# Graph network kernel: one wait in front of a group's eight matmuls, one release behind them, and the two paths as two `If`s

## The chip, the cores and the metric

The kernel runs on one core of one Trainium2 chip. The metric is the device time of one execution in microseconds (us). The engines are named as the profile names them: PE multiplies matrices, PEld is its weight load, DVE and ACT are the vector and the scalar engine, POOL is GpSimd, SP issues most of the plain transfers. A trailing q (SPq, POOLq, DVEq) is an engine's own instruction queue.

## What is computed

Four graph layers follow one another on 6250 nodes with 256 features and 100000 edges, sorted by destination. Cut to what matters:

```python
h = relu(layernorm(x)); x = x + L0(h)   # 8-head attention over edges, then a feed-forward part
h = relu(layernorm(x)); x = x + L1(h)   # msg = h[src] * filter(edge); sum by dst; two projections
h = relu(layernorm(x)); x = x + L2(h)   # one-head attention over edges
h = relu(layernorm(x)); x = x + L3(h)   # graph convolution: sum of h[src] by dst, scaled, plus bias
```

Each layer gathers one table row for every edge by `src` and sums the rows, weighted, by `dst`.

## The kernel before

**Groups.** The edges are cut into G = 98 groups of 1024. A group is J = 8 tiles of 128 edges. For every tile one indirect DMA, issued by POOL (`gather`, line 129; its line in the profile is L130), brings 128 table rows from DRAM into SBUF. Then eight matmuls add the eight tiles up in one PSUM tile, by multiplying the rows with a one-hot matrix that says which of 128 neighbouring nodes an edge ends at. Each float32 matmul shows as two passes in the profile, so a group's sum is 16 entries. The sums of overlapping node windows are then put together for each block of 128 nodes (`sum_block`), and the block goes on through the layer's dense part.

**Four stages.** There is one loop over the groups for each layer; the text calls them stages 0 to 3.

- Stage 0 (lines 792 to 827): `rows0` (L184) gathers into slices of `xbuf`, NV = 6 groups deep; `logits0` (L746) reads a column of all eight tiles, L816 multiplies the rows in place by the attention values on DVE, `one_hot0` (L731) and `one_hot_t` (L725, the instruction at L729) build one-hot tiles, and `sum_window` (L666, matmul L670) sums. `rows0` of the first four groups stands before the branch.
- Between stages 0 and 1 lies the feed-forward part (`feed_forward` and lines 831 to 921), with no gathers.
- Stage 1 (lines 978 to 1036): gathers go into slices of `big`, NH = 12 groups deep. `filters` (L954) makes three PSUM tiles of edge filters on PE (L960), for tiles 0 to 2, 3 to 5 and 6 to 7; three DVE multiplications (L1005) put them on the rows; the matmuls (L1008) sum. Then DVE works on the edge features (`ea`, L1010 and L1011), on the block that is done (`out1`, L971), on `row` (L1026), on the next one-hot (`one_hot1`, L968) and adds the sum to `agg` (L1035).
- Stage 2 (lines 1108 to 1121): `rows2` (L1049) gathers into a pool of five buffers; `one_hot2` (L1064) reads a column of all eight tiles (L1068), takes an exponential on ACT (L1072) and builds eight scaled one-hot tiles (L1075); `sum_window` sums; `out2` (L1079) and `table3_row` (L1101) finish a block.
- Stage 3 (lines 1143 to 1160): gathers go into a pool of six buffers; the matmuls (L1154) take the tiles in the order 7, 6, ..., 0; the one-hot tiles (`one_hot3`, L1127, instruction L1130) are built one group ahead; `end3` (L1134) writes the result.

**What sets the order.** Inside `tc.manual_schedule()` each engine runs its instructions in the order of the code. Engines are held to each other by semaphores alone. The framework places a wait wherever an instruction reads what another engine or a DMA wrote, or writes where another still reads. It tracks slices: a gather into tile j of `xbuf` or `big` waits for the matmul that read tile j some groups before, and matmul j waits for gather j and for the DVE instruction that wrote what it reads. The gathers use eight DMA semaphores in turn, so a group's eight gathers have eight different ones. Buffers from a pool (stages 2 and 3) are given back as a whole, after the last reader. POOL issues nothing but gathers in the loops, so it runs ahead of the other engines as far as the buffers allow.

**The two paths.** At line 309 a flag is read into a register, `general`, on every engine. Lines 1444 to 1449 run `fast()`, described above, when it is 0, and else `slow()`, a general version. With these inputs the fast path runs. Inside it a smaller `If` (L1058) guards a rare case and is not taken.

Of the kernel before, what the change touches and what calls it, by code (L numbers as in the profile page):

```python
# [13 lines left out]
OP = mybir.AluOpType  # L14
# [3 lines left out]
P = 128  # L18
J = 8
W = 128  # L20
D = 256
H = 8
HD = D // H
FF = 512
FL = 128
VR = D + H + 1
TR = D + 2
# [8 lines left out]
def tile_gnn(ctx: ExitStack, tc: tile.TileContext, a: dict, out: bass.AP, N: int):  # L36
# [11 lines left out]
    nc = tc.nc  # L48
# [78 lines left out]
        nc.vector.reciprocal(o, o)  # L127

    def gather(rows, table, idx, j):
        nc.gpsimd.indirect_dma_start(  # L130
            out=rows, out_offset=None, in_=table,
            in_offset=bass.IndirectOffsetOnAxis(ap=idx[:, j:j + 1], axis=0))

    def norm_stats(b0, b1):
        for b in range(b0, b1):
# [45 lines left out]
    AHEAD = 4  # L181
    vrows = [xbuf[:, i * J * VR:(i + 1) * J * VR].rearrange("p (j r) -> p j r", j=J) for i in range(NV)]

    def rows0(g):  # L184
        for j in range(J):
            gather(vrows[g % NV][:, j, :], vt, src_i[:, g * J:(g + 1) * J], j)

    sct = dram.tile([NP, 2 * H], F32, name="sct")
    with ExitStack() as l0:
# [455 lines left out]
    def fast():  # L645
# [17 lines left out]

            return [(g, HW * g - OFF - P * b) for g in range(max(0, 2 * b - 1), min(G, 2 * b + 3))]

        def sum_window(pool, oh, rows, n):  # L666

            s = ps("S", [P, n])
            for j in range(J):
                nc.tensor.matmul(s, oh[:, j, :], rows[:, j, :], start=j == 0, stop=j == J - 1)  # L670
            ws = pool.tile([P, n], F32, name="ws", bufs=6)
            nc.scalar.activation(ws, s, AF.Copy)  # L672
            return ws

        def sum_block(sums, b, n):

# [21 lines left out]
        with tc.tile_pool(name="e0", bufs=2) as ep:  # L698

            scw = ep.tile([P, NB, 2, 2 * H], F32, name="scw", bufs=1)  # L700
            for odd in range(2):
                for b0, b1 in ((0, 32), (32, NB)):
# [6 lines left out]
                    else:  # L709
# [5 lines left out]
            place = ep.tile([P, G], F32, name="place", bufs=1)  # L715
            nc.gpsimd.iota(place, pattern=[[HW, G]], base=-OFF, channel_multiplier=1,
                           allow_small_or_imprecise_dtypes=True)
            sums, drows, tos, dgs, ohs, vs, ms, mts = {}, {}, {}, {}, {}, {}, {}, {}

            def loads0(g):  # L720
                if g < G:
# [9 lines left out]
            def one_hot0(g):  # L731
                if g < G:
                    ohs[g] = ep.tile([P, J, P], F32, name="oh")
                    for j in range(J):
                        nc.vector.tensor_scalar(ohs[g][:, j, :], iota, rel[:, g * J + j:g * J + j + 1],
                                                None, OP.is_equal)

            def of_dst(g):

# [52 lines left out]
            with tc.manual_schedule():  # L792
                for g in range(2):
                    loads0(g)
                one_hot_t(0)
                one_hot0(0)
                of_dst(0)
                for g in range(G + 2):
                    vg = vrows[g % NV]
                    if AHEAD <= g < G:  # L800
                        rows0(g)
                    loads0(g + 2)
                    for b in blocks_done(g):
                        vs[b] = ep.tile([P, H, HD], F32, name="v")
                        nc.sync.dma_start(vs[b], vt[b * P:(b + 1) * P, 0:D].rearrange("p (h c) -> p h c", c=HD))
                    if g == 6:
                        made(of1)
                    if g == 8:
                        made(of2)
                    summed = [(b, sum_block(sums, b, VR)) for b in blocks_done(g - 1)]  # L810
                    projected = [(b, project0(b)) for b in blocks_done(g - 2)]
                    if g < G:
                        ex = logits0(g)
                        one_hot_t(g + 1)
                        vals = vg[:, :, 0:D].rearrange("p j (h c) -> p j h c", c=HD)
                        nc.vector.tensor_tensor(vals, vals, ex[:, :, :, None].to_broadcast([P, J, H, HD]),  # L816
                                                OP.mult)
                    of_dst(g + 1)
                    for b, s in summed:
                        attn0(b, s)  # L820
                    if g < G:
                        sums[g] = sum_window(ep, ohs[g], vg, VR)
                    for b, s in summed:
                        turn0(b)
                    one_hot0(g + 1)
                    for b, t in projected:
                        residual0(b, t)
# [103 lines left out]
        with tc.tile_pool(name="e1", bufs=2) as ep, Psum("ps1", S=2, A=3, B=1, C=1, K=1) as ps:  # L931
# [5 lines left out]
                nc.sync.dma_start(wr3[33 * i + 32:33 * i + 33, i, :], a["L1_gnn_b_r2m"][None, :])  # L937

            agg = ep.tile([P, HW * (G - 1) + P], F32, name="agg", bufs=1)
            rbs, eas, ohs, parts, normed = {}, {}, {}, {}, {}  # L940

            def loads(g):

# [10 lines left out]
            def filters(g):  # L954

                parts[g] = []
                for q in range(3):
                    n = min(3, J - 3 * q)
                    t = ps("A", [P, n, FL])
                    nc.tensor.matmul(t, rbs[g][0:33 * n, g % 2, q, :], wr3[0:33 * n, 0:n, :],  # L960
                                     start=True, stop=True)
                    parts[g].append((slice(3 * q, 3 * q + n), t))

            def one_hot1(g):
# [13 lines left out]
            with tc.manual_schedule():  # L978
# [6 lines left out]
                for g in range(G + 2):  # L985
                    hg = hgs[g % NH]
                    if g < G:
                        for j in range(J):
                            gather(hg[:, j, :], ht1, src_i[:, g * J:(g + 1) * J], j)
                    loads(g + 2)  # L990
                    added = []
                    for b in blocks_done(g - 1):
# [8 lines left out]
                            nc.tensor.transpose(t[:, k, :], normed[b][:, k * P:(k + 1) * P], ident)  # L1001
                        turned.append((b, t))
                    if g < G:
                        for js, t in parts[g]:
                            nc.vector.tensor_tensor(hg[:, js, :], hg[:, js, :], t, OP.mult)  # L1005
                        s = ps("S", [P, P])
                        for j in range(J):
                            nc.tensor.matmul(s, hg[:, j, :], ohs[g][:, j, :], start=j == 0, stop=j == J - 1)  # L1008
                        ea = eas[g]
                        nc.vector.tensor_tensor(ea, ea, wa[:, None, :].to_broadcast([P, J, FL]), OP.mult)  # L1010
                        nc.vector.tensor_reduce(te[:, g * J:(g + 1) * J], ea, AX.X, OP.add)  # L1011
# [32 lines left out]
        brow = on_all(wp, "L3_gnn_b", D)  # L1044
        bufs2, ahead = 5, 4
        with tc.tile_pool(name="e2", bufs=2) as ep:
            vgs, sums, normed = {}, {}, {}

            def rows2(g):  # L1049
                vgs[g] = ep.tile([P, J, TR], F32, name="vg", bufs=bufs2)  # L1050
                for j in range(J):
                    gather(vgs[g][:, j, :], xt2, src_i[:, g * J:(g + 1) * J], j)

            with tc.manual_schedule():
                for g in range(ahead):
# [8 lines left out]
            def one_hot2(g):  # L1064

                gs = slice(g * J, (g + 1) * J)
                al = ep.tile([P, J], F32, name="al")
                nc.vector.tensor_tensor(al[:, :, None], vgs[g][:, :, D:D + 1], te[:, gs][:, :, None], OP.add)  # L1068
                leaky(al, al, 0.01)
                nc.vector.tensor_tensor(al, al, shift[:, gs], OP.subtract)  # L1070
                ex = ep.tile([P, J], F32, name="ex")
                nc.scalar.activation(ex, al, AF.Exp)  # L1072
                oh = ep.tile([P, J, P], F32, name="oh")
                for j in range(J):
                    nc.vector.tensor_scalar(oh[:, j, :], iota, rel[:, g * J + j:g * J + j + 1],  # L1075
                                            ex[:, j:j + 1], OP.is_equal, OP.mult)
                return oh

            def out2(b, s):  # L1079

# [27 lines left out]
            with tc.manual_schedule():  # L1108
                for g in range(G + 2):
# [2 lines left out]
                    summed = [(b, sum_block(sums, b, TR)) for b in blocks_done(g - 1)]  # L1112
                    turned = [(b, turned2(normed[b])) for b in blocks_done(g - 2)]
                    if g < G:
                        oh = one_hot2(g)
                    for b, s in summed:
                        normed[b] = out2(b, s)
                    if g < G:
                        sums[g] = sum_window(ep, oh, vgs[g], TR)
                    for b, hb in turned:  # L1120
                        table3_row(b, hb)

# [1 line left out]
        with tc.tile_pool(name="e3", bufs=2) as ep, tc.manual_schedule():  # L1124
            sums = {}

            def one_hot3(g):  # L1127
                oh = ep.tile([P, J, P], F32, name="oh")
                for j in range(J):
                    nc.vector.tensor_scalar(oh[:, j, :], iota, rel[:, g * J + j:g * J + j + 1], None,  # L1130
                                            OP.is_equal)
                return oh

            def end3(b, s):  # L1134
                r0, r1 = b * P, min(N, (b + 1) * P)
# [4 lines left out]
                if r1 > r0:  # L1140
                    nc.sync.dma_start(out[r0:r1, :], y[0:r1 - r0, :])

            oh = one_hot3(0)
            for g in range(G + 1):
                if g < G:
                    vg = ep.tile([P, J, D], F32, name="vg", bufs=6)
                    for j in range(J):
                        gather(vg[:, j, :], xt3, src_i[:, g * J:(g + 1) * J], j)
                summed = [(b, sum_block(sums, b, D)) for b in blocks_done(g - 1)]
                if g < G:  # L1150

                    s = ps("S", [P, D])
                    for j in range(J):
                        nc.tensor.matmul(s, oh[:, J - 1 - j, :], vg[:, J - 1 - j, :], start=j == 0, stop=j == J - 1)  # L1154
                    if g + 1 < G:
                        oh = one_hot3(g + 1)
                    sums[g] = ep.tile([P, D], F32, name="ws", bufs=6)
                    nc.scalar.activation(sums[g], s, AF.Copy)
                for b, s in summed:
                    end3(b, s)  # L1160
# [280 lines left out]
                if r1 > r0:  # L1441
                    nc.sync.dma_start(out[r0:r1, :], y[0:r1 - r0, :])

    with tc.If(general < 1) as path:
        with ExitStack() as fctx:
            fast()
    with path.Else():
        with ExitStack() as fctx:
            slow()

# [53 lines left out]
```

## Time and profile before

| | us |
|---|---|
| five runs: median (lowest to highest) | 4511.63 (4508.82 to 4512.8) |
| the profiled execution: its own time | 4513.57 |
| the profiled execution: span from first to last instruction | 4511.8 |
| busy: PE / POOL / PEld / DVE / ACT | 3129.7 / 3070.7 / 2393.0 / 2102.2 / 624.1 |
| stage 0, from the start of its first gather to the end of its last | 180.4 to 1204.5 |
| stage 1, likewise | 1496.1 to 2479.3 |
| stage 2, likewise | 2498.6 to 3492.9 |
| stage 3, likewise | 3510.7 to 4496.4 |
| mean granted PE clock | 0.806 of full speed |

A line of groups reads: line, engine, operation, output<-inputs, count | busy us, mean ns of one | idle us just before them, and what ended most of that idle time. A line of the timeline reads: start, duration in us, engine, line, operation, count, and in brackets the idle time before it and who ended it. A line of waits reads: who waited for whom, us in total, times, longest in us. The busy time of POOL in a gather is the time that the engine spends on issuing it; the rows land later.

### The profile page before, as it was taken

How to read it: one execution, taken by the hardware profiler on the slowest of the kernel's cores; microseconds unless marked ns; L12 is line 12 of the kernel's file. 1: busy time of each engine (PE TensorE's matmuls, PEld its weight loads, DVE VectorE, ACT ScalarE, POOL GpSimd, SP SyncE). 2: the span in 40 equal slices, each digit the busy share in tenths (PEclk: the TensorE clock that was granted, in tenths of full speed). 3: DMA queues.
4: the chain of work that ended last, by engine and by line, in shares of the span. 5: the costliest groups of instructions: out<-in, count | busy, mean ns of one | idle time of the engine just before them, and what ended most of it. 6: DMA issues, size and time to landing. Idle time of an engine off the chain costs nothing.

```text
span 4511.8 us, 42644 instructions
## 1 busy us (share of the span) xinstructions
PE 3129.7 (69%) x12132; PEld 2393.0 (53%) x12133; DVE 2102.2 (47%) x6391; ACT 624.1 (14%) x1559; POOL 3070.7 (68%) x3215
## 2 busy tenths in 40 slices
PE   7689888888897666666666566666666556566565
PEld 4377777777645544445545344545444444444444
DVE  5476655565524566666767333333333222222222
ACT  3211010010124100000000122222222000000000
POOL 0377777777501677777777677777777677777776
PEclk9888888888898777777777787878778787787888
DMA  3355555555500444444444344444444333333333
GB/s 105 114 178 169 161 160 159 161 162 161 153 0 15 117 122 126 123 129 125 123 126 115 89 111 112 112 111 112 111 112 111 96 112 111 111 112 111 111 111 100
DMA packets 258746, 536.81 MB, mean 119 GB/s; under 512 B 65096, under 2 KB 144966, under 8 KB 258502
## 3 DMA queue, kind: packets, MB, share of 16 engines
q0 software_dynamic: 137984, 364.28, 29.3%
q1 hardware_dynamic: 107750, 156.85, 11.4%
q10 hardware_dynamic: 12768, 12.85, 0.9%
q8 instruction: 103, 1.69, 0.2%
q14 instruction: 141, 1.16, 0.1%
HBM read 504.57 MB, written 29.15 MB: 118 GB/s over the span
## 4 chain that ended last, share of the span: by engine, by line
PE 33%; POOL 28%; issue 15%; DMA 12%; DVE 9%; ACT 2%; DVEq 0%; POOLq 0%; ACTq 0%; SPq 0%
POOL vg L130 24%; PE ps_S L670 13%; DMA big<-ht,src_i 6%; PE ps_A L743 5%; DMA xbuf<-vt,src_i 3%; PE ps_S L1008 3%; DMA vg<-xt,src_i 3%; POOL big L130 2%; PE ps_A L441 2%; PE ps_B L447 2%; DVE oh L968 2%; PE ps_Q L245 2%; PE ps_T L680 1%; PE ps_S L1154 1%; DVE ea L1010 1%
## 5 line engine op out<-in xcount | busy, mean ns | idle before, releaser
L130 POOL DMA_INDIRECT vg<-xt,src_i x1568 | 1498.0, 955 | 519.1 <-issue 480.9
L130 POOL DMA_INDIRECT xbuf<-vt,src_i x784 | 785.3, 1002 | 241.2 <-issue 103.8
L130 POOL DMA_INDIRECT big<-ht,src_i x784 | 744.4, 949 | 245.0 <-issue 130.6
L1154 PE MATMUL ps_S<-vg,oh 128*128 128x256 f32 x1568 | 514.3, 500 | 399.6 <-DMA vg<-xt,src_i 393.4
L670 PE MATMUL ps_S<-vg,oh 128*128 128x258 f32 x1568 | 476.9, 470 | 326.5 <-DVE oh L1075 320.1
L1154 PEld LDWEIGHTS ps_S<-vg,oh 128*128 128x128 f32 x1568 | 397.6, 260 | 516.6 <-issue 369.1
L670 PEld LDWEIGHTS ps_S<-vg,oh 128*128 128x128 f32 x1568 | 368.8, 241 | 424.1 <-DVE oh L1075 353.0
L1130 DVE TENSOR_SCALAR oh<-iota,rel 128x128 f32<-128x128 f32 x784 | 166.5, 302 | 746.2 <-PE ps_S L1154 743.1
L670 PE MATMUL ps_S<-xbuf,oh 128*128 128x265 f32 x1568 | 492.9, 480 | 14.0 <-issue 13.0
L1008 PE MATMUL ps_S<-oh,big 128*128 128x128 f32 x1568 | 315.5, 370 | 245.0 <-DVE big L1005 144.9
L1008 PEld LDWEIGHTS ps_S<-oh,big 128*128 128x128 f32 x1568 | 283.4, 272 | 280.6 <-DVE big L1005 161.0
L670 PEld LDWEIGHTS ps_S<-xbuf,oh 128*128 128x128 f32 x1568 | 371.9, 243 | 102.2 <-issue 17.9
L743 PE MATMUL ps_A<-scw,to 128*128 128x16 f32 x1568 | 220.3, 284 | 115.9 <-DVE to L729 115.7
L743 PEld LDWEIGHTS ps_A<-scw,to 128*128 128x128 f32 x1568 | 216.3, 220 | 135.3 <-issue 89.3
L680 PE MATMUL ps_T<-ws,shifts 128*128 128x265 f32 (+2 forms) x1164 | 278.9, 382 | 0.0
L1075 DVE TENSOR_SCALAR oh<-iota,rel,ex 128x128 f32<-128x128 f32 x784 | 218.5, 372 | 94.4 <-ACT ex L1072 93.7
L960 PE MATMUL ps_A<-wr,rb 99*128 99x384 f32 (+1 forms) x588 | 241.3, 558 | 9.4 <-DMA rb<-in_rbf 9.4
L1068 DVE TENSOR_TENSOR al<-vg,te 128x8 f32<-128x8 f32 x98 | 16.4, 167 | 484.1 <-DMA vg<-xt,src_i 484.1
L680 PEld LDWEIGHTS ps_T<-ws,shifts 128*128 128x128 f32 x1164 | 220.7, 190 | 33.9 <-ACT ws L672 0.3
L1005 DVE TENSOR_TENSOR big<-big,ps_A 128x384 f32<-128x384 f32 (+1 forms) x294 | 139.8, 507 | 207.8 <-DMA big<-ht,src_i 198.0
L816 DVE TENSOR_TENSOR xbuf<-xbuf,ps_E 128x2048 f32<-128x2048 f32 x98 | 223.6, 2282 | 25.1 <-ACT ps_E L754 25.1
L672 ACT ACTIVATE ws<-ps_S 128x265 f32<-128x265 f32 (+1 forms) x196 | 75.6, 386 | 1062.8 <-PE ps_S L670 1062.8
(228 smaller groups left out, 3328.9 us busy)
## 6 DMA issues: line engine op xcount, KB each, us to landing
drow<-in_dst_row SPq DMA_DIRECT2D x98, 512.0 KB
ea<-in_edge_attr SPq DMA_DIRECT2D x98, 512.0 KB
vg<-xt,src_i POOLq DMA_INDIRECT x1568, 2.8
xbuf<-vt,src_i POOLq DMA_INDIRECT x784, 3.5
big<-ht,src_i POOLq DMA_INDIRECT x784, 2.7
rb<-in_rbf SPq DMA_DIRECT2D x196, 49.5 KB
vt<-row SPq DMA_DIRECT2D x49, 132.5 KB
xt<-row SPq DMA_DIRECT2D x49, 129.0 KB
```

Of the source, the lines that this page charges most:

```text
L130: nc.gpsimd.indirect_dma_start(out=rows, out_offset=None, in_=table, in_offset=bass.IndirectOffsetOnAxis(ap=idx[:, j:j + 1], axis=0))
L245: nc.tensor.matmul(qk, hbs[b][:, k, :], wqk[:, k, :], start=k == 0, stop=k == 1)
L670: nc.tensor.matmul(s, oh[:, j, :], rows[:, j, :], start=j == 0, stop=j == J - 1)
L680: nc.tensor.matmul(t, shift_by(s), sums[g], start=i == 0, stop=i == len(parts) - 1)
L743: nc.tensor.matmul(dgs[g][:, j, :], tos[g][:, j * P:(j + 1) * P], scw[:, g // 2, g % 2, :], start=True, stop=True)
L816: nc.vector.tensor_tensor(vals, vals, ex[:, :, :, None].to_broadcast([P, J, H, HD]), OP.mult)
L960: nc.tensor.matmul(t, rbs[g][0:33 * n, g % 2, q, :], wr3[0:33 * n, 0:n, :], start=True, stop=True)
L1005: nc.vector.tensor_tensor(hg[:, js, :], hg[:, js, :], t, OP.mult)
L1008: nc.tensor.matmul(s, hg[:, j, :], ohs[g][:, j, :], start=j == 0, stop=j == J - 1)
L1075: nc.vector.tensor_scalar(oh[:, j, :], iota, rel[:, g * J + j:g * J + j + 1], ex[:, j:j + 1], OP.is_equal, OP.mult)
L1130: nc.vector.tensor_scalar(oh[:, j, :], iota, rel[:, g * J + j:g * J + j + 1], None, OP.is_equal)
L1154: nc.tensor.matmul(s, oh[:, J - 1 - j, :], vg[:, J - 1 - j, :], start=j == 0, stop=j == J - 1)
```

## The change

The diff, cut to its core:

```diff
+    def wait_for(ins, *earlier):
+        for e in earlier:
+            tc.add_manual_dep(ins.ins, e.ins.name, SYNC, reason="one wait for a group's tiles")
+        return ins
...
     def rows0(g):
-        for j in range(J):
-            gather(vrows[g % NV][:, j, :], vt, src_i[:, g * J:(g + 1) * J], j)
+        landed[g] = [wait_for(gather(vrows[g % NV][:, j, :], vt, src_i[:, g * J:(g + 1) * J], j),
+                              *([summed0[g - NV]] if g - NV in summed0 else []))
+                     for j in range(J)]
...
+        def sum_tiles(s, pairs, made, got):
+            for j, (l, r) in enumerate(pairs):
+                m = wait_for(nc.tensor.matmul(s, l, r, start=j == 0, stop=j == len(pairs) - 1), made)
+                if j == 0:
+                    wait_for(m, *got)
+            return m
...
-                        for j in range(J):
-                            gather(hg[:, j, :], ht1, src_i[:, g * J:(g + 1) * J], j)
+                        got = [wait_for(gather(hg[:, j, :], ht1, src_i[:, g * J:(g + 1) * J], j),
+                                        *([summed1[g - NH]] if g >= NH else []))
+                               for j in range(J)]
...
-                        for js, t in parts[g]:
-                            nc.vector.tensor_tensor(hg[:, js, :], hg[:, js, :], t, OP.mult)
+                        for i, (js, t) in enumerate(parts[g]):
+                            made_g = nc.vector.tensor_tensor(hg[:, js, :], hg[:, js, :], t, OP.mult)
+                            wait_for(made_g, filtered[g], *(() if i else got))
...
-                    for j in range(J):
-                        nc.tensor.matmul(s, oh[:, J - 1 - j, :], vg[:, J - 1 - j, :], start=j == 0, stop=j == J - 1)
+                    sum_tiles(s, [(oh[:, j, :], vg[:, j, :]) for j in range(J)], made_g, got)
...
-    with tc.If(general < 1) as path:
+    with tc.If(general < 1):
         with ExitStack() as fctx:
             fast()
-    with path.Else():
+    with tc.If(general > 0):
         with ExitStack() as fctx:
             slow()
```

In all four stages the first matmul of a group now waits for all eight gathers and for the last DVE instruction that makes the group's operands: L816 in stage 0, the third L1005 in stage 1, the eighth one-hot tile in stages 2 and 3. In stages 0 and 1 every gather of a group waits for the last matmul of the group that had its buffer, not for the matmul of its own tile. In stage 1 the first of the three multiplications (L1005) waits for all eight gathers, and all three wait for the last of the group's filter matmuls. In stage 3 the matmuls go in the order 0 to 7. At the end, the choice between the paths is made by two branches on the same register: after the fast path every engine meets a second `If`, whose body it skips. No arithmetic is added or removed, and no transfer changes.

## The prediction

> **What bounds the kernel now.** The page's first part shows PE at 69% and POOL at 68% of the span, which says little, so I went to the groups of instructions for POOL.
>
> ```profile
> L130 POOL DMA_INDIRECT vg<-xt,src_i x1568 | 1498.0, 955 | 519.1 <-issue 480.9
> L130 POOL DMA_INDIRECT xbuf<-vt,src_i x784 | 785.3, 1002 | 241.2 <-issue 103.8
> L130 POOL DMA_INDIRECT big<-ht,src_i x784 | 744.4, 949 | 245.0 <-issue 130.6
> ```
>
> A gather holds POOL for about 0.95 us and about 0.3 us of idle time stands before it. Whether that idle time is a wait that could be removed is the question of this case. The waits of POOL inside stage 1 answer it:
>
> ```profile
> POOL big L130 <- issue: 129.6, 425, 0.3
> POOL big L130 <- PE ps_S L1008: 50.3, 165, 0.3
> POOL big L130 <- DMA big<-ht,src_i: 29.6, 97, 0.3
> ```
>
> Each row divided by its count is 0.305 us (129.6/425, 50.3/165, 29.6/97), and the longest is 0.3. The gap is the same whether nothing, a matmul or a DMA is named as its end. In stage 3, where a buffer is given back as a whole, the row "issue" has 235.7 us in 773 gathers, again 0.305. The gap is part of issuing; no semaphore lengthens it. Next, the stretches from a stage's first gather to its last:
>
> ```profile
> 180.40:1204.50 1024.10, 858.15 (x4011) 716.73 (x4012) 620.78 (x1727) 99.74 (x341) 785.52 (x785) 0.83 0.56 168
> ...
> 1496.10:2479.30 983.20, 647.64 (x2524) 483.91 (x2524) 665.28 (x1649) 58.08 (x238) 744.36 (x784) 0.75 0.46 125
> ...
> 2498.60:3492.90 994.30, 611.39 (x2207) 481.63 (x2207) 350.99 (x1406) 248.69 (x475) 750.92 (x784) 0.79 0.41 111
> ...
> 3510.70:4496.40 985.70, 591.34 (x1934) 466.02 (x1934) 227.09 (x912) 37.25 (x97) 746.99 (x784) 0.79 0.38 111
> ```
>
> The columns after the length are busy us of PE, PEld, DVE, ACT and POOL, the granted clock, the DMA share, GB/s. Stage 1 is 784 x (0.949 + 0.305) = 983.1 us, its whole length. POOL issues gathers back to back in every stage, 3987 us in all, and never waits for a buffer. PE and DVE follow it with slack: 858 us of PE in 1024 us, less in the others. So a wait that is shorter or longer on PE or DVE doesn't show in the middle of a stage; it shows only behind a stage's last gather, where a chain runs until the next stage can gather.
>
> **One thing does slow POOL.** The gathers of stage 0 take 1002 ns, those of stage 1 949: 784 x 0.053 = 41.6 us. The timeline of a group in stage 0 shows where it is from:
>
> ```profile
> 1133.37 0.22 DVE L751 TENSOR_TENSOR al<-xbuf,ps_A 128x64 f32<-128x64 f32 x1 [3.90 <-DMA xbuf<-vt,src_i]
> ...
> 1134.03 0.75 DVE L729 TENSOR_SCALAR to<-drow,place 128x1024 f32<-128x1024 int32 x1
> ...
> 1134.23 1.36 POOL L130 DMA_INDIRECT xbuf<-vt,src_i  x1 [0.30 <-PE ps_B L780]
> ```
>
> A gather that starts while L729 runs takes 1.36 us, 0.41 more. L729 follows L751, which waits for the landing of all eight gathers; that is so after the change too, so the phase stays, and this price with it.
>
> **The change part by part.**
>
> *Gather waits (stages 0 and 1).* A gather waits for the last matmul of six or twelve groups before, some 60 or 120 us behind POOL. The gap stays 0.305. Gain and loss 0.
>
> *Stage 0.* The first matmul waits for L816, as it effectively did: L816 writes all eight tiles in one instruction, and the landings come before it. Eight waits on DMAs now stand in front of the first matmul instead of one before each. Waiting instructions of PE stand 0.08 to 0.11 us apart in the trace (185.29, 185.40, 185.48). Two semaphores to one, that is four, 0.3 us if they come last, and as much less for the later seven. I take +0.2 at the stage's end, bounds -0.3 and +0.3.
>
> *Stage 1.* These lines follow the last gather (it ends at 2479.29):
>
> ```profile
> 2451.05 1.35 DVE L1005 TENSOR_TENSOR big<-big,ps_A 128x384 f32<-128x384 f32 x3
> ...
> 2481.11 0.42 DVE L1005 TENSOR_TENSOR big<-big,ps_A 128x256 f32<-128x256 f32 x1 [1.55 <-DMA big<-ht,src_i]
> 2481.58 0.71 PE L1008 MATMUL ps_S<-oh,big 128*128 128x128 f32 x4 [1.04 <-DVE big L1005]
> 2486.23 0.21 DVE L1035 TENSOR_TENSOR agg<-agg,ps_S 128x64 f32<-128x64 f32 x1
> ```
>
> Now only the third L1005 comes after the last landing. After the change all three do: 1.35 instead of 0.42 us, and four waiting DVE instructions in front of them (about 0.07 each). DVE is the chain here (L1010, L1011, `out1`, then L1035), so L1035 comes 0.93 + 0.28 = 1.2 us later. The sum now starts behind the third L1005, near 2482.8. Its 16 passes take 3.75 us (2469.64, unbroken), to 2486.5, before L1035 at 2487.4: hidden. If the passes ran at the 6.1 us of stage 2's slowest sums, L1035 would wait until about 2489 and the end be 2.8 late; if DVE is a us behind as well, 4. I take +1.2, bounds 1.1 and 4. In the middle, queued behind the waiting L1005 on DVE is all its work of the group. An even group then needs 1.35 + 3.75 + 1.93 (L1020) + 0.43 (`row`) + 2.15 (one-hots) + 0.2, near 10 us; an odd one, on DVE alone, 1.35 + 2.4 + 2.0 + 2.15 + 0.2, 8.1 us. Together 18 us of the 20.1 that two groups of gathers take. It fits.
>
> *Stage 2.* L1068 already waits for all eight gathers.
>
> ```profile
> 3495.85 2.14 DVE L1075 TENSOR_SCALAR oh<-iota,rel,ex 128x128 f32<-128x128 f32 x8 [0.34 <-ACT ex L1072]
> 3496.25 3.75 PE L670 MATMUL ps_S<-vg,oh 128*128 128x258 f32 x16 [0.17 <-DVE oh L1075]
> ...
> 3510.67 0.98 POOL L130 DMA_INDIRECT vg<-xt,src_i  x1 [17.77 <-DVE oh L1130]
> ```
>
> The sum starts beside the one-hots, 0.40 us after they begin; it would start at their end, 3498.0 or a little later: +1.7, all of it on the way to stage 3's first gather. Bounds 1.3 and 2.7 (a colder PE).
>
> *Stage 3.* With the order 7 to 0 the first matmul waits for the last gather already. The other waits, 0.3 us, move in front of it: +0.3, bounds -0.1 and 0.5.
>
> *The second branch.* The trace has the untaken `If` of L1058: it cost DVE 1.12 us (idle before L1070), and made POOL wait 5.0 us, for its own gathers. At the end of the fast path, SP issues the last output until 4506.97, branches at 4507.02 and goes on at 4509.58; it then passes 13 waiting instructions 0.065 apart, most of them while that output lands (until about 4510.7). With a second `If` SP has to set its semaphores right behind that landing and pass the 13 after it: about +0.9. Bounds 0.1 and 5.0 (POOL's wait, if nothing hid it; its last gather has landed by 4498.5, 12 us before).
>
> *Gathers against DVE.* The phase of DVE's work in stage 1 moves. What a one-hot or an `xn` costs a gather it falls on:
>
> ```profile
> 3480.34 0.41 DVE L1090 TENSOR_SCALAR xn<-xbuf,mv,rstd 128x256 f32<-128x256 f32 x1
> 3480.50 1.07 POOL L130 DMA_INDIRECT vg<-xt,src_i  x1 [0.30 <-issue]
> ```
>
> That is 0.12; gathers that start in a run of one-hots take 1.00 to 1.01 (3488.14, 2514.88), 0.06. Over a floor of 0.947 stage 1 has 744.36 - 742.4 = 1.9 us of this, stage 2, whose one-hots all follow the last landing, 8.5, of which 37 gathers behind L1090 make 4.4. I take stage 2 without them: 4.1 - 1.9 = +2.2. Bounds: all of the 1.9 goes; or every group has two gathers in the one-hots and every block one behind L975, 98 x 2 x 0.06 + 49 x 0.12 = 17.6.
>
> SBUF — State Buffer (section Who interferes with whom) of the Trainium skill says that a `tensor_scalar` in a two-port mode and a GpSimd instruction lock each other out for the whole instruction. By an estimate from that rule a run of eight one-hots could hold gathers for much of its 2 us, over 100 us in 98 groups; the 0.06 above speaks against taking it so, though L729's 0.41 agrees with it.
>
> **The sum.** 0.2 + 1.2 + 1.7 + 0.3 + 0.9 + 2.2 = +6.5 us. On the profiled execution: span 4518.3, own time 4513.57 + 6.5 = 4520.1. That execution lies 1.9 us above the median of the five runs; theirs becomes 4518.1. The bounds add to 0 and +30, but not all ends come together.
>
> **The rivals.**
>
> 1. *DVE and PE become the bound in stage 1.* The early L1005 let DVE and PE overlap; now they stand in series. For it: PEclk is lowest there, 0.75, and L960 takes 1.9 us in one group and 3.4 in another. Against it: 18 of 20.1 us. If the sum takes 5.0 us, an even group needs 11.1 and an odd one, with L960 at 3.4, 1.35 + 5.0 + 3.4 = 9.8: 20.9, 0.8 more than the gathers for two groups; 49 pairs lag 39 us, and the stage's end comes that much later: 4557. It decides from 4.6 us a sum. TensorE: Matmul & The Clock Gate (section HAM oscillation — how this bites in real kernels) warns that idle gaps over some 3.4 us put PE back to half its clock; by an estimate from it a sum would take 7.5 us and this rival would win, but no row here ties the clock to a gap. Chance 0.08.
> 2. *The lock of L729 goes.* If the eight landings reached DVE 0.6 us earlier or later, L729 would miss the gather and stage 0 lose up to 41.6 us: 4470 to 4500. L751's wait isn't touched, so 0.05.
> 3. *Nothing shows.* The tails are hidden by the next stage's preparation and the waits cost what they did: 4511.6, 0.12.
>
> **How the numbers follow.** The forecast has 0.75: within it 4510 to 4528. 0.2% of the time, 9.0 us, is what a measurement tells from no change, so slower means above 4520.7 and faster below 4502.6. Of the forecast's 0.75 I put 0.21 above 4520.7 (contention or the end near their upper bounds) and 0.54 within. Faster: 0.05. Same: 0.54 + 0.12 = 0.66. Slower: 0.21 + 0.08 = 0.29. The range 4509 to 4529 holds the forecast and the third rival and leaves out about 0.15.
>
> **What would show it.** Right: gaps of 0.305 before all gathers; stages 1 to 3 still 983 to 995 us long; from the last gather of stage 1 to the first of stage 2 about 20.5 instead of 19.3, of stage 2 to stage 3 19.5 instead of 17.8; from the last gather to the end of the span 16.6 instead of 15.4; stage 0's gathers near 1002 ns. Wrong: a gather of stage 1 that waits over 0.3 us, a stage whose length moves by over 10 us, or 1.36 us gathers gone.

## The result and the profile after

The changed kernel takes 4513.70 us (median of 24 runs, 4508.65 to 4518.88), the kernel before in the same comparison 4511.64 (44 runs, 4506.55 to 4515.93). The ratio is 1.0005 with a 95% interval of 0.9999 to 1.001: +2.3 us, -0.5 to +4.5. The forecast was +6.5, in the class "within 0.2%".

The profiled execution of the changed kernel has an own time of 4502.69 and a span of 4500.9, 10.9 us below that of before, against the sign of the medians; that own time lies below all 24 runs of the median. The groups of POOL's gathers tell why (columns: count | busy us, mean ns | idle before).

```profile
L130 POOL DMA_INDIRECT vg<-xt,src_i x1568 | 1487.8, 949 | 521.5 <-issue 486.2
L130 POOL DMA_INDIRECT xbuf<-vt,src_i x784 | 782.8, 998 | 241.1 <-issue 211.9
L130 POOL DMA_INDIRECT big<-ht,src_i x784 | 742.5, 947 | 245.2 <-issue 196.0
```

Every group is 2 to 6 ns a gather shorter. Take the 20th percentile of a stage's gathers as its floor, what an undisturbed one takes: it was 0.943 to 0.946 us in the profiled execution of before and is 0.941 to 0.944 here. 0.003 us times 3136 gathers is 9 us. A second profile of the unchanged kernel (e3 below) shows 0.941 to 0.944 as well and a span of 4494.3, so this is not the change's. The median gather tells the same: 0.947 to 0.949 us by stage in the first profile of before, 0.944 to 0.946 in all eleven later profiles of any kernel. The times follow: in the comparison of the first profile the unchanged kernel took 4506.55 to 4515.93 us, in those of the experiments, on chips 6 and 4, 4494.12 to 4502.85. Whether the chip makes this difference isn't shown. **One profiled span beside another can't carry an effect of 2 us here; its parts can.** Those are the gaps, the boundaries between stages, and what gathers take over their floor.

The waits of POOL in stage 1 (us in total, times, longest):

```profile
POOL big L130 <- issue: 193.9, 636, 0.3
POOL big L130 <- DVE big L1026: 14.6, 48, 0.3
POOL big L130 <- DMA big<-ht,src_i: 12.8, 42, 0.3
```

193.9/636, 14.6/48 and 12.8/42 are 0.305 again, with other names beside it: the new waits on the last matmul of an older group lengthen no gap. The stretches of stage 1, 2 and 3 and the boundaries behind them (length, then busy us of PE, PEld, DVE, ACT and POOL, granted clock, DMA share, GB/s):

```profile
1494.20:2475.40 981.20, 586.30 (x2516) 462.78 (x2516) 663.85 (x1647) 58.57 (x237) 742.48 (x784) 0.78 0.46 125
2475.40:2495.90 20.50, 11.19 (x35) 6.81 (x35) 11.31 (x30) 1.98 (x8) 0.05 (x1) 0.61 0.07 19
2495.90:3480.80 984.90, 603.13 (x2201) 482.02 (x2201) 350.40 (x1406) 243.49 (x475) 743.63 (x784) 0.83 0.41 112
3480.80:3502.10 21.30, 14.62 (x55) 10.86 (x53) 9.49 (x41) 5.61 (x13) 0.02 (x1) 0.82 0.08 26
3502.10:4484.80 982.70, 589.87 (x1934) 464.90 (x1934) 226.81 (x913) 37.17 (x97) 744.18 (x784) 0.80 0.39 111
4484.80:4500.90 16.10, 6.63 (x22) 5.27 (x22) 1.73 (x4) 0.38 (x1) 0.00 (x0) 0.77 0.10 29
```

Stage 1 is 784 x (0.947 + 0.305) = 981.6 us long: still POOL's own time. The boundaries grew: 19.3 to 20.5 us, as foretold; 17.8 to 21.3, where 19.5 was foretold; 15.4 to 16.1, where 16.6 was. Stage 2 is 9.5 us shorter: 7.3 in its gathers, and 2 at the untaken `If` inside it, where POOL waited 3.0 us instead of 5.0 (3.0 to 3.1 in all later profiles of either kernel, so this is not the change's). The end of stage 1, with the line numbers of the changed kernel (L1005 is L1026 now, L670 and L1008 are L681, L1035 is L1056):

```profile
2477.44 1.35 DVE L1026 TENSOR_TENSOR big<-big,ps_A 128x384 f32<-128x384 f32 x3 [1.64 <-DMA big<-ht,src_i]
2478.84 2.96 PE L681 MATMUL ps_S<-oh,big 128*128 128x128 f32 x16 [2.23 <-DVE big L1026]
2483.48 0.22 DVE L1056 TENSOR_TENSOR agg<-agg,ps_S 128x64 f32<-128x64 f32 x1
```

All three multiplications follow the landing, 1.35 us of them, and the sum ends at 2481.8, 1.7 us before L1056 could use it: hidden, as worked out. The end of stage 2 (L1072 is L1092, L1075 is L1095, L672 is L691):

```profile
3477.18 6.75 PE L681 MATMUL ps_S<-vg,oh 128*128 128x258 f32 x16 [5.82 <-DVE oh L1095]
...
3483.19 0.17 DVE L1090 TENSOR_TENSOR al<-al,shift 128x8 f32<-128x8 f32 x1
...
3483.97 0.39 ACT L691 ACTIVATE ws<-ps_S 128x258 f32<-128x258 f32 x1 [9.09 <-PE ps_S L681]
...
3484.84 0.47 ACT L1125 ACTIVATE big<-ps_C,dinv 128x256 f32<-128x256 f32 x1 [0.48 <-PE ps_C L1124]
3485.21 0.20 ACT L1092 ACTIVATE ex<-al 128x8 f32<-128x8 f32 x1
3485.44 2.14 DVE L1095 TENSOR_SCALAR oh<-iota,rel,ex 128x128 f32<-128x128 f32 x8 [2.08 <-ACT ex L1092]
...
3487.64 3.75 PE L681 MATMUL ps_S<-vg,oh 128*128 128x258 f32 x16 [1.10 <-DVE oh L1095]
```

In the trace of before, the same place on ACT:

```profile
3493.51 0.39 ACT L672 ACTIVATE ws<-ps_S 128x258 f32<-128x258 f32 x1 [6.59 <-PE ps_S L670]
...
3494.38 0.47 ACT L1105 ACTIVATE big<-ps_C,dinv 128x256 f32<-128x256 f32 x1 [0.48 <-PE ps_C L1104]
...
3495.60 0.21 ACT L1072 ACTIVATE ex<-al 128x8 f32<-128x8 f32 x1 [0.75 <-DVE al L1070]
```

Two things are late. The last sum starts 2.20 us after its one-hots begin, 0.40 before: +1.8. And the one-hots begin late: `al` is ready at 3483.36, but its exponential starts at 3485.21, where before it took 0.1 us to follow. It stands in ACT's queue behind `big` and the copy (`ws`) of the sum of group 96, which waited for its own last one-hot too and ended at 3483.9. That is the other 1.75 us.

### The profile page after: what moved, and what is told of

Its sections match the earlier page's. It is cut to its first block, busy times and chain, and to the rows that moved or that the text cites. A ratio compares the mean times of both kernels' runs of the same rounds, so it can differ in the third digit from the quotient of the medians.

```text
span 4500.9 us, 42030 instructions
## 1 busy us (share of the span) xinstructions
PE 3062.5 (68%) x12132; PEld 2375.8 (53%) x12133; DVE 2103.3 (47%) x6391; ACT 619.1 (14%) x1559; POOL 3056.0 (68%) x3215
## 5 line engine op out<-in xcount | busy, mean ns | idle before, releaser
L681 PE MATMUL ps_S<-vg,oh 128*128 128x258 f32 (+1 forms) x3136 | 990.4, 485 | 779.7 <-DMA vg<-xt,src_i 407.1
L681 PEld LDWEIGHTS ps_S<-vg,oh 128*128 128x128 f32 x3136 | 764.2, 250 | 998.1 <-issue 387.6
L681 PE MATMUL ps_S<-oh,big 128*128 128x128 f32 x1568 | 309.2, 378 | 340.0 <-DVE big L1026 315.1
L681 PE MATMUL ps_S<-xbuf,oh 128*128 128x265 f32 x1568 | 490.1, 478 | 13.2 <-issue 12.5
L681 PEld LDWEIGHTS ps_S<-oh,big 128*128 128x128 f32 x1568 | 287.0, 283 | 370.6 <-DVE big L1026 247.8
L681 PEld LDWEIGHTS ps_S<-xbuf,oh 128*128 128x128 f32 x1568 | 369.8, 242 | 100.5 <-issue 16.7
L1095 DVE TENSOR_SCALAR oh<-iota,rel,ex 128x128 f32<-128x128 f32 x784 | 214.5, 369 | 144.6 <-ACT ex L1092 144.6
L691 ACT ACTIVATE ws<-ps_S 128x265 f32<-128x265 f32 (+1 forms) x196 | 76.3, 389 | 1224.2 <-PE ps_S L681 1224.2
L1026 DVE TENSOR_TENSOR big<-big,ps_A 128x384 f32<-128x384 f32 (+1 forms) x294 | 132.3, 505 | 228.3 <-DMA big<-ht,src_i 227.4
L980 PE MATMUL ps_A<-wr,rb 99*128 99x384 f32 (+1 forms) x588 | 209.1, 495 | 10.1 <-DMA rb<-in_rbf 10.1
L988 DVE TENSOR_SCALAR oh<-iota,rel,cut 128x128 f32<-128x128 f32 x784 | 211.6, 360 | 0.0
L900 POOL TENSOR_TENSOR xbuf<-xbuf,bout 128x1024 f32<-128x1024 f32 (+1 forms) x13 | 29.0, 2227 | 256.4 <-ACT xn L898 249.6
```

The source lines that it names most:

```text
L681: m = wait_for(nc.tensor.matmul(s, l, r, start=j == 0, stop=j == len(pairs) - 1), made)
L900: nc.gpsimd.tensor_tensor(x[:, b0:b1, :], x[:, b0:b1, :], w1["bout"][:, None, :].to_broadcast([P, b1 - b0, D]), OP.add)
L980: filtered[g] = nc.tensor.matmul(t, rbs[g][0:33 * n, g % 2, q, :], wr3[0:33 * n, 0:n, :], start=True, stop=True)
L988: nc.vector.tensor_scalar(ohs[g][:, j, :], iota, rel[:, c], w1["cut"][:, c], OP.is_equal, OP.mult)
L1026: made_g = nc.vector.tensor_tensor(hg[:, js, :], hg[:, js, :], t, OP.mult)
L1095: made_g = nc.vector.tensor_scalar(oh[:, j, :], iota, rel[:, g * J + j:g * J + j + 1], ex[:, j:j + 1], OP.is_equal, OP.mult)
```

## The experiments

Each is the kernel before with one edit, unless said otherwise, and its time stands beside that of the kernel before on the same chip. The table has the parts of the profiled executions that the verdicts rest on, in us: the boundaries from last to first gather, what the 784 gathers of stage 2 take over their floor, and the time from the end of the last output's DVE instruction (L1139) to the start of the program's last instruction, 0.05 us before the span's end. Each row is one profiled execution.

| kernel | stage 1 to 2 | stage 2 to 3 | stage 2 over floor | last output to end |
|---|---|---|---|---|
| before | 19.28 | 17.77 | 9.5 | 5.13 |
| e3, before again | 19.22 | 17.50 | 6.7 | 5.17 |
| e5, order only | 19.28 | 17.13 | 7.1 | 5.15 |
| e10, landings in stage 2 | 19.11 | 18.25 | 8.1 | 4.95 |
| e1, two branches | 19.36 | 17.13 | 7.3 | 6.74 |
| e9, all waits in stage 2 | 19.38 | 20.54 | 5.2 | 4.94 |
| e2, all waits, one branch | 19.90 | 20.95 | 4.6 | 5.39 |
| after | 20.46 | 21.32 | 5.1 | 5.84 |
| e6, after, with the order | 20.16 | 20.42 | 4.7 | 6.02 |

**The branches alone (e1_branches).**

```diff
-    with tc.If(general < 1) as path:
+    with tc.If(general < 1):
...
-    with path.Else():
+    with tc.If(general > 0):
```

> Only the second part of the change: the kernel before with the two paths as two Ifs. Theory (POOL's issuing sets the length of every stage, the change acts only behind the last gather): stages unchanged, the stretch from the last gather to the end of the span 0.5 to 1.0 us longer than the 15.4 of before, time +0.3 to +1.0 us, a ratio of 1.0001 to 1.0002. Rival (gain and loss cancel: the waits bring some us, the branch takes them back): +4 us or more.

4499.19 against 4500.26 us, ratio 1.0003 (0.9994 to 1.0012). The clock can't tell it from nothing; the end of its timeline can, in a span of 4497.3:

```profile
4484.12 3.69 PE L1154 MATMUL ps_S<-vg,oh 128*128 128x256 f32 x16 [1.95 <-DMA vg<-xt,src_i]
...
4490.14 0.42 DVE L1139 SCALAR_TENSOR_TENSOR y<-ps_T,xbuf 128x256 f32<-128x256 f32 x1
```

The DVE work ends at 4490.56, and the last column of the table has 6.74 us from there, in the single-branch kernels 4.94 to 5.39. The whole tail behind the last gather is 15.4 in both, and reading only that would hide the branch: here the last sum took 3.69 us, in the profile of before 5.38. The interval of the times reaches to +5.4 us and doesn't exclude the rival's +4; the table does, since the rest of this row is near those of the kernel before. Over the table's three kernels with two branches the end takes 6.20 on average, over the six with one 5.12: **+1.1 us**, with a scatter of 0.9 and 0.5 within the two sets.

**The waits alone (e2_waits): after, with one branch again.**

```diff
-    with tc.If(general < 1):
+    with tc.If(general < 1) as path:
...
-    with tc.If(general > 0):
+    with path.Else():
```

> Only the first part: all the waits of the change, with If and Else as before. Theory: the stretches between the stages grow by 0.3, 1.2 and 3.5 us as in the changed kernel, the gathers lose some us of blocking by DVE in stage 2; together 0 to +6 us, tail as before (15.4, plus 0.3 at most). Rival (the waits bring a gain that the branch takes back): -3 us or lower.

4502.11 us, ratio to before 1.0005 (0.9995 to 1.0014): +1.9 us, within the theory's 0 to +6, and the rival's -3 lies outside the interval. The two longer boundaries and the shorter stage 2 come with the waits; the end is near the others of one branch.

**The kernel before, profiled again (e3_before_again).** No edit.

> The kernel before, unchanged, for a second profile. Theory: the floor of a gather (0.945 us before, 0.942 after) differs from execution to execution with no change in the program, so here it may be anything from 0.940 to 0.950 and the span 4495 to 4515; the blocked gathers come from the phase of DVE against POOL, which the program sets, so stage 2 again has some 37 gathers near 1.07 behind the xn of a block and some 8 us over its floor. Rival (the waits made the gathers faster): the floor is 0.945 again, and only the changed kernel has 0.942.

Span 4494.3, own time 4496.1. Stage 0 takes 1020.65, stage 1 980.61, stage 3 982.38: 3 us shorter each than in the first profile, with the same work. The theory of the floor held; in stage 2, though, 17 gathers are held by over 0.1 us and 6.7 us lie over the floor, fewer than expected. The unchanged kernel's median was 4511.64, 4500.26 and 4497.73 us in the three comparisons with several runs.

**What holds a gather in stage 0 (e4_no_lock_before).**

```diff
-                    nc.vector.tensor_scalar(tos[g], drows[g], place[:, g:g + 1], None, OP.is_equal)
+                    nc.vector.tensor_tensor(tos[g], drows[g], place[:, g:g + 1].to_broadcast([P, J * P]), OP.is_equal)
```

> The kernel before with L729 as a tensor_tensor against a broadcast column in place of a tensor_scalar; same result. Theory (the 1.36 us gathers are POOL held by that one instruction, and POOL's issuing is the bound): no gather of 1.36 us in stage 0 any more, stage 0 near 984 to 990 us, time -30 to -42 us. Rival A (an instruction with two SBUF inputs holds the gather as well): gathers still 1.36 or longer, 0 to +30 us. Rival B (stage 0 is near a bound of PE, 858 us busy of 1024, so the shorter gathers only expose PE): stage 0 stays above 1010 us, gaps of POOL over 0.3 us appear, -10 us at most.

4539.00 against 4500.26 us, ratio 1.0091 (1.0077 to 1.0105). My theory of the lock fell: the other form of instruction holds gathers too, and for longer, since it takes 1.22 us. The group's mean, and two places of the timeline:

```profile
L130 POOL DMA_INDIRECT xbuf<-vt,src_i x784 | 825.3, 1053 | 241.1 <-issue 131.5 <-PE ps_S L670 71.0 <-PE ps_A L743 14.0
```

```profile
1127.61 1.22 DVE L729 TENSOR_TENSOR to<-drow,place 128x1024 f32<-128x1024 int32 x1
1127.77 1.87 POOL L130 DMA_INDIRECT xbuf<-vt,src_i  x1 [0.30 <-issue]
...
1138.77 0.95 POOL L130 DMA_INDIRECT xbuf<-vt,src_i  x1 [0.30 <-issue]
1138.98 1.22 DVE L729 TENSOR_TENSOR to<-drow,place 128x1024 f32<-128x1024 int32 x1
```

Where L729 is running when the gather starts, the gather takes 1.87 us. Where L729 starts 0.21 us after the gather, the gather takes 0.95. For this form of L729, what decides is who is first, not that two overlap: none of the ten gathers that start 0.1 to 0.6 us ahead of it takes over 0.98 us. The 38.7 us lie above rival A's 0 to 30.

**L729 moved ahead (e5_order_before, and e6_order_after on the changed kernel).** The next group's one-hot goes ahead of `leaky`, right behind L751.

```diff
                 nc.vector.tensor_tensor(al, vg[:, :, D:D + H], dg[:, :, 0:H], OP.add)
+                one_hot_t(g + 1)
                 leaky(al, al, 0.2)
...
                         ex = logits0(g)
-                        one_hot_t(g + 1)
```

> The kernel before with L729 one step earlier on DVE: behind L751, ahead of the leaky slope, so that it begins 0.5 us sooner against the gathers. Nothing else changes. Theory (a gather is held only if the locking instruction runs when the gather starts; L729 then ends 0.0 to 0.2 us into it): gathers of 1.36 us go, excess of stage 0 over its floor falls from 43 us to 5 to 15 us, time -28 to -38 us. Rival A (any overlap of L729 with a gather holds it): excess stays above 35 us, time within 5 us. Rival B (PE and DVE then set stage 0): POOL gaps over 0.3 us and -10 us at most.

> The same move of L729 in the changed kernel. Theory: -28 to -38 us against the kernel before, plus the 0 to 4 us of the changed waits. Rivals as for the kernel before.

4472.28 us on the kernel before, ratio 0.9941 (0.9928 to 0.9955), and 4473.66 on the changed one, 0.9950 (0.9937 to 0.9964), against 4497.73. These are the fastest versions here, and the change adds as little to the first (1.4 us) as to the kernel before. 25.5 us instead of the 28 to 38 of the theory: the time over the floor in stage 0 fell from 43.8 to 17.6 us, not to 5 to 15.

```profile
1107.54 0.22 DVE L751 TENSOR_TENSOR al<-xbuf,ps_A 128x64 f32<-128x64 f32 x1 [3.08 <-DMA xbuf<-vt,src_i]
...
1107.68 0.93 DVE L729 TENSOR_SCALAR to<-drow,place 128x1024 f32<-128x1024 int32 x1
...
1108.40 1.02 POOL L130 DMA_INDIRECT xbuf<-vt,src_i  x1 [0.30 <-issue]
...
1117.30 1.33 POOL L130 DMA_INDIRECT xbuf<-vt,src_i  x1 [0.30 <-issue]
...
1117.77 0.75 DVE L729 TENSOR_SCALAR to<-drow,place 128x1024 f32<-128x1024 int32 x1
```

L729 now begins about 0.5 us earlier and ends 0.2 us into the gather, which costs that gather 0.07; the gather at 1117.30 is one of 13 that are still held for over 0.3 us. It is held although L729 starts 0.47 us after it, and ends 0.12 us behind L729; so the theory, that only an instruction running at the gather's start holds it, does not cover this form (see the last section).

**A wait in the middle of a stage (e7_one_group_late).** In stage 3 the first matmul of a group waits for the gathers of the next group as well.

```diff
+                got = []
+                if h < G:
+                    vg = vgs3[h] = ep.tile([P, J, D], F32, name="vg", bufs=6)
+                    got = [gather(vg[:, j, :], xt3, src_i[:, h * J:(h + 1) * J], j) for j in range(J)]
+                g = h - 1
...
                     for j in range(J):
-                        nc.tensor.matmul(s, oh[:, J - 1 - j, :], vg[:, J - 1 - j, :], start=j == 0, stop=j == J - 1)
+                        m = nc.tensor.matmul(s, oh[:, J - 1 - j, :], vg[:, J - 1 - j, :], start=j == 0, stop=j == J - 1)
+                        if j == 0:
+                            wait_for(m, *got)
```

> The kernel before with a much longer wait: in stage 3 the first matmul of a group waits for the gathers of the next group too, so every sum runs some 10 us later. Theory (a wait in the middle of a stage costs nothing while POOL finds its buffers free): stage 3 keeps its length within 3 us, only the end grows by one more sum behind the last landing, +5 to +8 us, ratio 1.001 to 1.002. Rival (each wait of PE is paid): 98 x 5 us or more, +500 us.

```profile
3498.38:4481.14 982.76, 584.74 (x1910) 459.79 (x1910) 226.88 (x910) 36.87 (x96) 744.24 (x784) 0.79 0.38 111
4481.14:4501.53 20.39, 11.70 (x46) 9.72 (x46) 2.70 (x6) 0.77 (x2) 0.00 (x0) 0.83 0.08 24
```

97 sums wait about 10 us longer each and the stage keeps its length, 982.8; only the tail grows, to 20.4 from the 13.5 to 16.1 of the table's kernels. The time is 4505.16, ratio 1.0018 (1.0009 to 1.0028). In this stage a wait costs where the gathers end, and nowhere else.

**Seven gathers of eight (e8_seven_gathers).**

```diff
-                    for j in range(J):
+                    for j in range(1, J):
                         gather(vg[:, j, :], xt3, src_i[:, g * J:(g + 1) * J], j)
...
-                    for j in range(J):
-                        nc.tensor.matmul(s, oh[:, J - 1 - j, :], vg[:, J - 1 - j, :], start=j == 0, stop=j == J - 1)
+                    for j in range(J - 1):
+                        nc.tensor.matmul(s, oh[:, J - 1 - j, :], vg[:, J - 1 - j, :], start=j == 0, stop=j == J - 2)
```

> The kernel before without the first of the eight gathers and matmuls of each group in stage 3, so that part of that layer's sum is left out. Theory (the length of a stage is the number of gathers x 1.254 us): -98 x 1.25 = -120 to -124 us. Rival (landing, PE or DVE set the pace, POOL only happens to be busy): less than half of it.

4375.74 against 4497.73 us, ratio 0.973 (0.9715 to 0.9745): 122.0 us for 98 gathers less, 1.245 each, and a gather with its gap is 0.945 + 0.305 = 1.25. The edit takes a landing and a matmul away with every gather, so alone it doesn't tell POOL from these; that no gap in that stage is over 0.32 us in any run, and that e7 delays every sum at no cost inside the stage, does.

**The waits of stage 2, taken apart (e9_stage2_all_waits, e10_stage2_landing_waits).** One profiled execution of each. e10 has `gots[g]` alone as the last argument.

```diff
-                        sums[g] = sum_window(ep, oh, vgs[g], TR)
+                        sums[g] = sum_window(ep, oh, vgs[g], TR, [made_g, *gots[g]])
...
                 nc.tensor.matmul(s, oh[:, j, :], rows[:, j, :], start=j == 0, stop=j == J - 1)
+                if j == 0:
+                    wait_for(m, *earlier)
```

> The kernel before; in stage 2 alone the first matmul of a group's sum waits for the eight landings and for the last of the eight one-hots. Theory (the last-one-hot wait makes the last two groups of stage 2 late, group 96 too, and group 96's late sum holds group 97's exponentials back in ACT's queue): from the last gather of stage 2 to the first of stage 3 20.8 to 21.4 us, as with the whole change (21.3), 17.8 before; the time of stage 2's gathers over their floor about 5 us, as with the whole change, 7 to 9.5 before; from stage 1 to stage 2 19.3 to 19.5, and 15.3 behind stage 3's last gather, as before. Rival (a part of the 3.5 us comes from what the change does elsewhere, the branches or the other stages' waits): 19.5, the 1.7 us of the one-hots alone.

> The kernel before; in stage 2 alone the first matmul of a group's sum waits for the eight landings, not for the last one-hot. Theory (the exponentials of a group wait for the landings already, so this wait is over before the first one-hot): stage 2 to stage 3 17.2 to 18.0 us, and 6.5 to 9.5 us of stage 2's gathers over their floor, both as before. Rival (it is the number of waits in front of the first matmul that costs): over 19 us.

Own times 4496.14 and 4499.17, beside 4495.70 of the kernel before. e9 gives 20.54 at the boundary and 5.2 us over the floor: the last-one-hot wait makes both, and the rest of the change isn't needed for either. It lies 0.3 under the range of the theory and 1.0 over the rival. Its timeline shows a smaller form of ACT's queue:

```profile
3480.07 0.39 ACT L681 ACTIVATE ws<-ps_S 128x258 f32<-128x258 f32 x1 [8.11 <-PE ps_S L677]
...
3480.36 0.17 DVE L1078 TENSOR_TENSOR al<-al,shift 128x8 f32<-128x8 f32 x1
...
3481.31 0.20 ACT L1080 ACTIVATE ex<-al 128x8 f32<-128x8 f32 x1
```

Here the sum of group 96 started as late as in the changed kernel but took 5.75 us instead of 6.75, and the exponential lost 0.8 us to ACT's queue instead of 1.85. e10 gives 8.1 us over the floor, as before, and 18.25, 0.25 over my range; its last sum starts 0.39 us after its one-hots begin, as before, so the waits on landings cost nothing there. Where the 0.25 comes from stays open.

## Why the prediction was right, and where it was not

The forecast's class and range held, with two terms of the sum far off in opposite directions. That they nearly cancel is luck: with stage 2's +3.3 alone put right, the sum would have been +8.1 instead of +6.5. By the table's means:

| term | forecast | measured |
|---|---|---|
| stage 1, all three L1005 behind the landing | +1.2 | +0.9 (19.27 to 20.17) |
| stage 2, the sum behind its one-hots | +1.7 | **+3.3** (17.56 to 20.81) |
| stage 3's waits | +0.3 | 0.0 (first matmul 2.12 instead of 2.08 behind the last gather) |
| the second branch | +0.9 | +1.1 |
| gathers against DVE | +2.2 | **-2.8** (7.7 to 4.9, in stage 2) |

Stage 0's +0.2 can't be seen: the boundary behind it is 291 to 293 us long in all the table's kernels. The five sum to +2.5, beside +2.3 (-0.5 to +4.5) of the medians.

*What bounds the kernel* was right, and is now shown for stage 3: a wait in the middle is free (e7), a gather less is worth 1.25 us (e8). No gap before a gather inside a stage moved in any run, but for the one at the untaken `If`.

*Stage 2, the step that failed:* "it would start at their end, 3498.0 or a little later: +1.7". I followed the last group alone, from its one-hots to its sum. The change delays the group before it too, and that one's copy to `ws` stands in ACT's in-order queue ahead of the last group's exponential. My trace had the rows, shown above: the copy of 96 at 3493.51, `big` behind it, and the exponential at 3495.60 after only 0.75 us of idle ACT. In the changed kernel the copy starts 3.2 us behind the stage's last gather instead of 0.6, and `big` with it, which eats this up. "Where the change adds a wait, name what is queued behind" has to be asked of the engines that wait for the waiter.

*The gathers against DVE:* I saw that the phase of DVE moves in stage 1 and gave stage 2 the part of a yardstick, the 4.4 us behind L1090 (`xn`) being left out as something that stays. Stage 1's figure over the floor went from 5.1 to 4.9, nothing. It was stage 2 that moved: its sum ends later, so `xn` comes later, and it no longer is running when the seventh gather starts. In the changed kernel, where `xn` is L1110:

```profile
3469.79 0.95 POOL L130 DMA_INDIRECT vg<-xt,src_i  x1 [0.30 <-issue]
3469.98 0.41 DVE L1110 TENSOR_SCALAR xn<-xbuf,mv,rstd 128x256 f32<-128x256 f32 x1
```

The prediction shows the same pair with `xn` 0.16 us ahead of the gather and 1.07 us for it. 40 gathers of stage 2 were held by over 0.1 us in the profile of before, 17 to 30 in those with its phase (e3, e5, e1, e10), and 5 to 8 in the four with the new one. e9 and e10 show that it is the wait for the last one-hot that does this. It is the only gain of the change. That it falls the right way is luck of 0.35 us.

*Rival 1, DVE and PE as the bound of stage 1,* didn't come, and for another reason than the one given. I said that no row ties PE's clock to a gap. Rows did. These are stage 2's sums of two groups in the changed kernel, the first after 1.10 us of idle PE, the second after 5.82 (the timeline's bracket), as stretches of PE (length, busy, granted clock, DMA share, GB/s):

```profile
3467.38:3471.13 3.75, 3.75 (x18) 1.00 0.41 108
...
3477.18:3480.18 3.00, 3.00 (x7) 0.50 0.34 89
3480.18:3483.93 3.75, 3.75 (x11) 0.58 0.27 70
```

The clock is granted at 1.00 or at 0.50 for most of a sum. In the trace of before, of the 98 sums of stage 2, the 48 after about 1 us of idle PE or less take 3.65 to 3.75 us, and the 49 after more than 5 us take 5.13 to 6.81 (so the 6.1 us that I called the slowest was not, which touches only an upper bound). TensorE: Matmul & The Clock Gate (HAM oscillation — how this bites in real kernels) of the Trainium skill has this rule, half the clock after idle over about 3.4 us. These rows agree; stage 3, below, doesn't, where the edge lies near 2.3 us, and there the measurement decides. But the estimate of 7.5 us a sum that I made from it doubled a time that was already that of half the clock: the 3.75 us at 2469.64 in the trace of before ran at a granted clock of 0.50, and in stage 1 of the changed kernel a sum takes 2.02 us at best and 3.79 at worst. So the point of 4.6 us, from which the rival decides, is out of reach.

*Rival 2* was right that L729 misses the gather if its phase moves by half a us: e5 made it so and took 25.5 us. It was right that this change doesn't do it, 43.0 us over the floor against 43.8. *Rival 3* gave a time 2 us from the median, yet its reason is wrong: the tails aren't hidden, they are paid and nearly given back.

The last sum of stage 3 takes 3.69 us in six of the table's kernels and 5.33 to 5.38 in before, e3 and after, which moves the tail by 1.7 whatever the change. That is the same clock: the granted clock was 1.00 in e1's sum, after 1.95 us of idle PE, and 0.68 in that of before, after 3.02. In stage 3 of the trace of before all 22 sums of at most 3.69 us follow 2.35 us of idle PE or less, and the 76 longer ones 2.35 or more; in the table's other kernels the two lengths part between 2.27 and 2.59. Why the idle time before the last sum differs is open.

## What to carry to other kernels

Where one engine issues back to back, price a new wait only at the ends of its stretches, and there follow two groups, not one, through the queues of every engine that waits for the delayed one. Then ask in every stage which DVE instruction will be running at the moment a gather starts, or for some of them soon after; half a microsecond there (e5) was worth more than all the waits together. When a change is small, split the trace into the parts that it can touch and compare each part over several kernels, since the unchanged kernel's span moved by 17.5 us between two profiles.

## What was not expected of the hardware

Whether DVE holds a gather depends on the instruction and on the moment. These counts are over all traces of this case; "held" means over 0.99 us.

- `xn` (L1090) holds gathers that start about 0.15 us or more behind its start. Of the 738 that start between 0.9 us before and 0.1 us behind it, none is held.
- L729 as a `tensor_tensor` (e4) holds, as in the lines above, all 92 gathers that start while it runs, from 0.05 us behind its start to 0.17 us before its end, and none of the ten that start 0.1 to 0.6 us ahead of it.
- L729 as a `tensor_scalar` holds all 953 gathers that start while it runs, over 0.1 us behind its start; nearly all of them end 0.81 to 0.83 us after it does. It also holds all 61 that start 0.13 to 0.45 us ahead of it; these end 0.12 us after it. Of the 221 that start 0.48 to 0.8 us ahead, 215 are not held.
- L816 runs for 2.28 us, and none of the 113 gathers that start within it in the trace of before takes over 0.96.

So a gather seems to be open to being held at two moments, one near its start and one in its middle, and the second only to some instructions; that is read from the times, and what happens at these moments isn't shown.

SBUF — State Buffer (Who interferes with whom) of the Trainium skill says that issue order, not the operation, decides who blocks. Taken as the order in which the two start, `xn` and e4 agree, and so does e5's L729 of 0.93 us behind a gather that began 0.53 us before it; the 61 gathers that came first and were held do not. The same section has a `tensor_tensor` with both inputs in SBUF contend with what GpSimd reads, and infers that it doesn't stall the making of descriptors; e4's gathers of 1.87 us that start while a `tensor_tensor` of 1.22 runs show that it can stall an indirect gather as a whole, at least with the broadcast column and the int32 input used here. Which part of the gather it stalls isn't shown.

The floor of a gather differs between two profiles of the same kernel, 0.943 to 0.946 us by stage in the first and 0.941 to 0.944 in e3. Over 3136 gathers that is 9 us, more than the change.
